# Planned order of shapes in attention, the last unit's sums on VectorE, and one expert per unit, in a two-layer transformer kernel

## The chip, the cores and the metric

The kernel runs on one core of a Trainium2 chip. The metric is device time in microseconds of one launch; lower is better. TensorE (PE) multiplies matrices, VectorE (DVE), ScalarE (ACT) and GpSimd (POOL) work on elements, SyncE (SP) and ACT issue most transfers. Each engine executes its own instructions in order.

## The reference, cut to what matters

Two layers over 2048 tokens of width 512, all in fp32.

```python
# layer 0
xn = layernorm(x)
q, k, v = heads(xn @ Wqkv + bqkv)              # 16 heads of 32
s = q @ k.T / sqrt(32) - slope[h] * (i - j)    # causal, slope[h] = 2 ** (-h / 2)
attn = softmax(s) @ v @ Wo + bo
e = argmax(softmax(xn @ Wg.T))                 # one of two experts per token
ffn = gelu(xn @ W0a.T + b0a) @ W0b.T + b0b if e == 0 else relu(xn @ W1a.T + b1a) @ W1b.T + b1b
x = x + attn + ffn                             # W0a, W1a: 1024 x 512
# layer 1
xn = layernorm(x)
x = x + lightning_attention(xn) + bitlinear_ffn(xn)   # linear attention with decays; 1408 wide, ternary weights
```

## The kernel before, in words

The kernel has four stages: attention of layer 0 (0 to 890 us), the experts of layer 0 (890 to 1157), the linear attention of layer 1 (1157 to 1552) and its ternary FFN (1552 to the end). The last two are the same in both kernels.

**Attention** has 16 units: four groups of four heads (`g`) by four blocks of 512 queries (`sb`). A unit has these parts on TensorE:
- `project` (L774, L886): queries, keys and values of the block. Q and K are split into two fp32r parts, written to DRAM and read back in another layout (SP, L834 and L847).
- `search` (L973): scores whose row maxima VectorE takes (L985). They are turned (L1039) and stored as `mr`.
- `attend`, once per block of 128 keys: `pick` (L1080) adds the negative maxima to four banks of PSUM, one for each head; `score` (L1090, on the diagonal also L1087) adds the scores; ScalarE takes the exponentials into `pT` (L1108); `weigh` (L1155) multiplies them with the values. The weighing of a key block comes after the scores of the next.
- `gather` (L1185): the exponentials of all key blocks are added up in `pT[0]`, on POOL. A product with ones (`sums`, L1202), two turns (L1237), a reciprocal and a multiplication divide the output.
- `out_proj` (L1305), in the last group only: the output projection, three groups as `others` and the last one as `late`; VectorE adds the result to the residual (L1314).

TensorE works in three shapes: `pick` uses 32 rows by 128 columns ("rows"), `weigh` and `sums` 128 rows by 32 columns ("columns"), the rest the whole 128x128 array ("full").

The order of attention is written by a planner when the kernel is built. `Plan` holds all parts as `Step`s, each with an engine, a duration, what it comes after, the PSUM banks or SBUF slots it takes, and a rank. TensorE's steps stand in streams (`own` for `attend`, `search`, `project`, `sums`, `others`, `late`, `extra`), in order within each. `choose` and `prefer` pick the next stream; `commit` sets the clock of the plan. `backlog` is the work waiting on VectorE, `searching` the work of searches already possible. There are seven PSUM banks beside `po`, and 18 SBUF slots (`homes`). An addition of `gather` may go to VectorE where POOL would start it later by more than `PATIENCE`. Steps up to the last weighing are then issued in the planned order on every engine (`manual_schedule`); those after it in an order that the compiler's scheduler chooses, mixed with the next stage.

**Experts.** `sort_tokens` gives each token a slot: tokens of expert 0 from the front, those of expert 1 from the end. Scatters (POOL) write the token numbers in this order to `sorted_tokens`; 18 gathers (L452, POOL) read them back to `take`. Nine units of 256 slots follow. Units that lie wholly among expert 0 or 1 use its weights; the slots of units above the border are shifted back by 256, so that the unit at the border is computed for either expert. Unit 0 is always expert 0, unit 8 always expert 1; the others load weights from `wa_all` and `wb_all`, copies of both experts behind each other in DRAM, at an index read from `second_i`. Per unit: gather and normalize the rows (L1557, L353; for units 0 and 1 as `xg_early` in attention), a first product (L1573, eight slices), ScalarE's activations (Relu L1580 and Gelu L1582, combined by VectorE in L1583; unit 0 has Gelu alone, L1577), a second product (L1587), the bias (L1589), a store to `expert_out`. After the last store POOL gathers its rows by `back` (L1694) for layer 1. While unit 0 is computed, `decay_tables` (L1489 to L1515) puts exponentials among its activations.

Of the kernel before, what the change touches and what calls it, by code (L numbers as in the profile page):

```python
# [9 lines left out]
F32 = mybir.dt.float32  # L10
I32 = mybir.dt.int32
# [6 lines left out]
P = 128  # L18
# [69 lines left out]
class Plan:  # L88
# [29 lines left out]
    def commit(self, step, at):  # L118
        if step.engine == "PE":
            shape = SHAPES.get(step.kind, "full")  # L120
            if shape != self.mode:
                at_work = step.took + (0.2 if self.mode == "rows" else 0.1)
                self.mode = shape
            else:
                at_work = step.took
        else:
            at_work = step.took
        end = at + at_work
# [44 lines left out]
    def prefer(self, ready, now):  # L173
# [12 lines left out]
        wanted = 1.2 if head is not None and head.kind in ("weigh", "pick") else 1.1  # L186
        search = ready.get("search")
        if search is not None and (search.kind == "turn" or backlog < wanted):
            return "search"
        if "sums" in ready and (head is None or self.mode == "columns" or head.kind == "pick"):  # L190
            return "sums"
        if "project" in ready and (ready["project"].kind == "middle" or self.searching() < 12.0):
            return "project"
        if "late" in ready and backlog < 1.0:
            return "late"
# [50 lines left out]
PATIENCE = 1.5  # L246
# [3 lines left out]
def block_kernel(  # L250
# [117 lines left out]

    dram = ctx.enter_context(tc.tile_pool(name="dram", bufs=1, space=bass.MemoryType.DRAM))
# [5 lines left out]
    expert_out = dram.tile([NU * LB, H], F32, tag="expert_out", name="expert_out")  # L375
# [4 lines left out]
    take = const.tile([P, NU, LB // P], I32, tag="take", name="take")  # L380
# [21 lines left out]
    def sort_tokens(pc, from_end):  # L402
# [22 lines left out]
        nc.vector.tensor_scalar(other, first0, -float(LB), float(LB), ALU.mult, ALU.add)  # L425
        nc.vector.tensor_tensor(other, other, pos, ALU.add)
# [3 lines left out]

        nc.vector.tensor_scalar(second[:, 0 : NU - 1], starts[:, 0 : NU - 1, 0], n0, None, ALU.is_gt)
        nc.vector.memset(second[:, NU - 1 : NU], 1.0)
        nc.vector.tensor_copy(second_i, second)
        shape = [P, NU, LB // P]
        slot = rt.tile(shape, F32, tag="slot", name="slot")
        nc.vector.tensor_scalar(slot[:, :, 0], second, -float(LB), None, ALU.mult)
        nc.vector.tensor_tensor(slot[:, :, 1], slot[:, :, 0], slots[:, :, 1], ALU.add)
        nc.vector.tensor_tensor(slot[:, :, 0], slot[:, :, 0], slots[:, :, 0], ALU.add)
        slot_i = rt.tile(shape, I32, tag="slot_i", name="slot_i")
        nc.vector.tensor_copy(slot_i, slot)  # L440
# [10 lines left out]
    def gather_take(u, k, slot_i):  # L451
        nc.gpsimd.indirect_dma_start(  # L452
            take[:, u, k : k + 1],
            None,
            sorted_tokens,
            bass.IndirectOffsetOnAxis(ap=slot_i[:, u, k : k + 1], axis=0),
        )

    starts = iota(const, [P, NU, 1], [[LB, NU], [0, 1]], 0, 0, "starts")
    slots = iota(const, [P, NU, LB // P], [[LB, NU], [P, LB // P]], 0, 1, "slots")  # L460
# [12 lines left out]
    with tc.tile_pool(name="psa", bufs=1, space=PSUM, reuse_waits="tile") as psa, tc.tile_pool(  # L473
# [582 lines left out]
        def attend(n, g, sb):  # L1056
# [120 lines left out]
            def gather(held_p):  # L1177

                for jb in range(1, nj):
                    cols = ds(first(jb), SB - first(jb))  # L1180

                    def step(jb=jb, cols=cols):
# [4 lines left out]
                    n_all = HPG * (SB - first(jb))  # L1187
                    added[jb] = add(
                        "POOL",
                        0.2 + 2.25e-3 * n_all,  # L1190
# [4 lines left out]
                        other=("DVE", 0.6 + 1.08e-3 * n_all),  # L1195
# [101 lines left out]
            def out_proj(il, groups):  # L1297
# [15 lines left out]
                def total():  # L1313
# [7 lines left out]
                    after=[d if last else others, wo["load"]] if il == 0 else [],  # L1321
# [22 lines left out]
        unit = {}  # L1344
        for n, (g, sb) in enumerate(units):
# [11 lines left out]
            for dst, src in copies[2 * (n - 4) : 2 * (n - 3)] if n >= 4 else []:  # L1357
                bulk(lambda dst=dst, src=src: nc.scalar.dma_start(out=dst, in_=src), after=[first_own[n]], rank=6)
# [17 lines left out]
        for i in range(NT):  # L1376
# [8 lines left out]
        taken = [  # L1385
            add("POOL", 1.0, lambda u=u, k=k: gather_take(u, k, t["slot_i"]), after=[step], rank=7, lag=7.0)
            for u in range(NU)
            for k in range(LB // P)
        ]
# [29 lines left out]
        def fetch_rows(i):  # L1419
            def step():  # L1420
                if i == 0:
                    early["xg"] = slot(held_g, "xg_early")
                u, k = divmod(i, LB // P)
                nc.gpsimd.indirect_dma_start(
                    early["xg"][:, i, :], None, x, bass.IndirectOffsetOnAxis(ap=take[:, u, k : k + 1], axis=0)
# [4 lines left out]
        def fetch_weights(k):  # L1430
            def step():
                w = slot(held_w[k], "wa_early", shape=[P, 2, F0])
                nc.sync.dma_start(out=w, in_=W0aT[ds(2 * k * P, 2 * P), :].rearrange("(c p) f -> p c f", p=P))
# [14 lines left out]
        for i in range(EARLY * (LB // P)):  # L1448
            fetched.append(
                add("POOL", 1.0, fetch_rows(i), after=[taken[i]] + used_up + fetched[-1:], rank=rank, lag=6.0, takes=[held_g] if i == 0 else [])  # L1450
            )
        weights = []
        for k in range(2):
            weights.append(add("SP", 0.62, fetch_weights(k), after=used_up + weights[-1:], rank=rank, takes=[held_w[k]]))
# [63 lines left out]
    with stage(4, 2, 2), tc.tile_pool(name="fc", bufs=1) as fc, tc.tile_pool(name="fw", bufs=2) as fw, tc.tile_pool(  # L1518
# [11 lines left out]
        for u in range(NU):  # L1530
            is0, is1 = firsts[:, u : u + 1], second[:, u : u + 1]
            wb = fw.tile([P, FC0, H], F32, tag="wb", name="wb")
            if u in (0, NU - 1):
                src_a, src_b = (W0aT, W0bT) if u == 0 else (W1aT, W1bT)
            else:
                e = nc.values_load(second_i[0:1, u : u + 1], engines=[mybir.EngineType.SP], min_val=0, max_val=1)
                src_a = wa_all[ds(e, 1)].rearrange("e k f -> (e k) f")
                src_b = wb_all[ds(e, 1)].rearrange("e f h -> (e f) h")
# [487 lines left out]
```

## Time and profile before

| | us |
|---|---|
| median of 3 runs | 1808.11 (1806.61 to 1808.33) |
| the profiled execution | 1807.18 |
| its span, first to last instruction | 1805.5 |
| attention | 0 to 890 |
| experts | 890 to 1157 |
| layer 1, linear attention | 1157 to 1552 |
| layer 1, FFN | 1552 to 1805.5 |

Durations of single instructions come from the profiled execution. Matrix instructions of fp32 appear in it as two passes, those of fp32r as one, so "x8" in a weighing is four instructions. Ends of TensorE's instructions are modelled; starts are recorded. In a row of the order of time the square bracket tells how long the engine was idle before it and what ended that.

### The profile page before, as it was taken

Reading aid. Unit: us, or ns where it says so; the run is one execution under the profiler, and the core shown is the slowest. Engines: PE = TensorE matmul, PEld = TensorE weight load, DVE = VectorE, ACT = ScalarE, POOL = GpSimd, SP = SyncE. Lnnn points to the kernel's source line nnn. Section 1 sums busy time; section 2 is a strip of 40 time slices with the busy share of each in tenths; the row PEclk is TensorE's granted clock in tenths of the full one; section 3 lists DMA queues with packets and bytes.
Section 4 is the critical chain, followed back from the end, with each engine's and each line's share of the span. In section 5 each row is a group of like instructions: output and inputs, shape, how many; then the busy total and the mean of one; then the engine's idle time right before and its main releaser. Section 6 shows DMA issues by size and latency. Waiting matters only on the chain.

```text
span 1805.5 us, 23633 instructions
## 1 busy us (share of the span) xinstructions
PE 1711.5 (95%) x9074; PEld 1086.6 (60%) x9074; DVE 892.0 (49%) x2116; ACT 697.0 (39%) x1223; POOL 805.2 (45%) x479
## 2 busy tenths in 40 slices
PE   5899999999999999899899999699999998799998
PEld 3656555555555555444556675476666664588886
DVE  3657656565666456621132231237766556652332
ACT  2344456555556556445152232123333331122221
POOL 8352879799967597879733130111111111000000
PEclk9899999999999999999999999899999998899999
DMA  7465243525442713301485453221210000310000
GB/s 207 152 198 158 54 94 101 140 53 147 119 145 88 213 39 100 111 1 65 128 302 188 169 175 111 73 76 60 73 48 30 13 1 1 98 49 6 24 24 24
DMA packets 90065, 173.94 MB, mean 96 GB/s; under 512 B 8944, under 2 KB 18176, under 8 KB 89696
## 3 DMA queue, kind: packets, MB, share of 16 engines
q1 hardware_dynamic: 74496, 133.33, 24.3%
q10 hardware_dynamic: 11088, 29.36, 4.8%
q0 software_dynamic: 4368, 9.75, 1.8%
q8 instruction: 71, 1.16, 0.3%
q14 instruction: 42, 0.34, 0.1%
HBM read 139.37 MB, written 41.43 MB: 100 GB/s over the span
## 4 chain that ended last, share of the span: by engine, by line
PE 44%; ACT 2%; DVE 2%; POOL 1%; issue 1%; DMA 1%; SPq 0%; DVEq 0%; ACTq 0%; POOLq 0%
PE ps_a L1950 9%; PE ps_c L1587 7%; PE ps_a L1715 7%; PE ps_a L1573 6%; PE ps_a L1857 3%; PE ps_a L1737 3%; PE ps_c L1935 2%; PE ps_b L1935 2%; PE ps_a L1814 1%; PE ps_a L1745 1%; PE ps_a L1811 1%; PE ps_a L1805 1%; DVE rms L1848 1%; PE ps_a L1845 1%; PE ps_a L1787 0%
## 5 line engine op out<-in xcount | busy, mean ns | idle before, releaser
L1185 POOL TENSOR_TENSOR pT<-pT 128x2048 f32<-128x2048 f32 (+3 forms) x144 | 553.1, 3843 | 106.9 <-ACT pT L1108 73.9
L985 DVE CUSTOM_DVE_ANT_0 bank<-bank,dist 128x512 f32<-128x512 f32 (+3 forms) x640 | 382.8, 631 | 183.4 <-PE bank L973 178.9
L1108 ACT ACTIVATE pT<-bank,kbias 128x512 f32<-128x512 f32 (+3 forms) x640 | 352.8, 624 | 179.8 <-PE bank L1090 156.5
L973 PE MATMUL bank<-Ks,Qs 128*128 128x512 f32 (+3 forms) x640 | 256.6, 440 | 8.1 <-DVE mx L985 6.8
L1090 PE MATMUL bank<-Qs,Ks 128*128 128x512 f32 (+3 forms) x640 | 213.9, 398 | 0.0
L973 PEld LDWEIGHTS bank<-Ks,Qs 128*128 128x128 f32 x640 | 113.8, 191 | 127.5 <-ACT pT L1108 48.0
L1950 PE MATMUL ps_a<-xs,w 128*128 128x512 f32 x704 | 168.2, 392 | 4.3 <-issue 4.3
L1950 PEld LDWEIGHTS ps_a<-xs,w 128*128 128x128 f32 x704 | 133.1, 189 | 33.0 <-issue 5.2
L1155 PE MATMUL po<-pT,v 128*32 128x512 f32 (+3 forms) x1280 | 150.7, 543 | 0.0
L1090 PEld LDWEIGHTS bank<-Qs,Ks 128*128 128x128 f32 x640 | 118.4, 190 | 32.6 <-issue 18.0
L774 PE MATMUL bank<-xnT,wqkv 128*128 128x512 f32 x256 | 127.7, 612 | 1.4 <-ACT xnT L714 1.4
L1587 PE MATMUL ps_c<-wb,hT 128*128 128x512 f32 x288 | 125.1, 592 | 0.0
L1715 PE MATMUL ps_a<-xn2T,wproj 128*128 128x256 f32 x512 | 118.4, 388 | 2.5 <-ACT xn2T L354 2.5
L1715 PEld LDWEIGHTS ps_a<-xn2T,wproj 128*128 128x128 f32 x512 | 96.9, 193 | 19.1 <-ACT xn2T L354 4.0
L1573 PE MATMUL ps_a<-xT,wa 128*128 128x256 f32 x448 | 98.3, 380 | 2.9 <-ACT xT L354 2.9
L1587 PEld LDWEIGHTS ps_c<-wb,hT 128*128 128x128 f32 x288 | 54.7, 190 | 65.0 <-issue 62.7
L1573 PEld LDWEIGHTS ps_a<-xT,wa 128*128 128x128 f32 x448 | 84.5, 190 | 15.1 <-ACT xT L354 3.9
L985 DVE DVE_READ_ACCUMULATOR2_ANT mx<- 128x1 f32 x640 | 90.7, 142 | 0.0
L1960 DVE TENSOR_TENSOR hf<-ps_a,s 128x512 f32<-128x512 f32 x44 | 30.4, 691 | 113.5 <-PE ps_a L1950 113.5
L1080 PE MATMUL bank<-mr,pick 32*128 32x512 f32 (+3 forms) x640 | 81.0, 464 | 5.5 <-DVE lo L815 2.8
L1836 POOL TENSOR_TENSOR sq<-og 128x512 f32<-128x512 f32 x16 | 16.9, 1059 | 152.4 <-DVE og L1831 152.4
L1848 DVE RECIPROCAL rms<-rms 128x512 f32<-128x512 f32 x16 | 53.6, 3351 | 57.5 <-ACT rms L1847 57.5
(228 smaller groups left out, 2209.2 us busy)
## 6 DMA issues: line engine op xcount, KB each, us to landing
Ks<-st SPq DMA_DIRECT2D x64, 256.0 KB, 4.6
Qs<-st SPq DMA_DIRECT2D x64, 256.0 KB, 4.5
wa<-wa_all SPq DMA_DIRECT2D x14, 1024.0 KB, 7.3
wb<-wb_all SPq DMA_DIRECT2D x14, 1024.0 KB, 7.9
xnT<-xn_dram ACTq DMA_DIRECT2D x12, 1024.0 KB, 5.7
raw<-in_L_ffn_w_dram SPq DMA_DIRECT2D x12, 704.0 KB, 4.1
st<-hi SPq DMA_DIRECT2D x32, 256.0 KB, 2.1
st<-lo SPq DMA_DIRECT2D x32, 256.0 KB, 2.0
```

Of the source, the lines that this page charges most:

```text
L774: nc.tensor.matmul(t["pp"], w3["w"][:, cc, ts(k, P)], xT["x"][:, cc, :], start=(cc == 0), stop=(cc == KC - 1),)
L973: nc.tensor.matmul(b["ps"][:, 0:w], un["Q"][:, hh, ts(il, P)], unit[n - sb + ch]["K"][:, hh, 0:w], start=True, stop=True,)
L985: nc.vector.tensor_tensor_reduce(out=b["ps"][:, 0:w], in0=b["ps"][:, 0:w], in1=c["dist"][:, ds(off, w)], scale=1.0, scalar=-3e38, op0=ALU.add,
L1080: nc.tensor.matmul(ps[hh][:, cols], c["pick"][hp, :], un["mr"][hp, cols], start=True, stop=False)
L1090: nc.tensor.matmul(ps[hh][:, cols], unit[n - sb + jb // TPS]["K"][:, hh, ts(jb % TPS, P)], un["Q"][:, hh, cols], start=False, stop=True,)
L1108: nc.scalar.activation(pT[jb][:, hh, cols], ps[hh][:, cols], AF.Exp, bias=c["kbias"][:, h, rel : rel + 1], scale=SLOPES[h],)
L1155: nc.tensor.matmul(t["po"][ts(hh, HD), cols], unit[n - sb + jb // TPS]["v"][:, jb % TPS, ts(hh, HD)], pT[jb][:, hh, cols], start=(jb == 0) ...
L1185: engine.tensor_tensor(acc, acc, pT[jb][:, :, cols], ALU.add)
L1573: nc.tensor.matmul(ph[:, 0:LB], wa[c][:, ts(f, P)], xT[:, c, :], start=(c == 0), stop=(c == KC - 1))
L1587: nc.tensor.matmul(po, hT[:, f, ts(k, P)], wb[:, f, :], start=(f == 0), stop=(f == FC0 - 1))
L1715: nc.tensor.matmul(pp[:, ts(i, LB)], w[:, c, ts(g, P)], self.xT[:, c, :], start=(c == 0), stop=(c == KC - 1),)
L1950: nc.tensor.matmul(pp, w[:, c, ts(f, P)], xs[i][:, c, :], start=(c == 0 and i == 0), stop=(c == KC - 1 and i == 1),)
```

## The change

1. *The planner.* A change of shape on TensorE costs 0.2 us in the plan where it leads to the full shape and 0.09 otherwise (before: 0.2 where it left rows, else 0.1). Where TensorE stands in columns and the next own step is a pick that can start within `WAIT` (0.4), nothing of another shape is put before it. The thresholds at which searches, projections and late products are preferred are others, and `PATIENCE` is 4.0 instead of 1.5.
2. *The last unit's additions* are given to VectorE.
3. *The experts.* Eight units of 256 slots are computed for one expert each, the one to which the slot in their middle belongs. The 128 slots at the border that this leaves out are a last unit of one tile. `sort_tokens` finds that tile (`meet`), its expert, and the place of its tokens (`back`). `take` is read by one load on SP and one gather. All units, unit 0 too, load weights at an index and have both activations.

```diff
     def commit(self, step, at):
+        end = at + step.took
         if step.engine == "PE":
+
             shape = SHAPES.get(step.kind, "full")
             if shape != self.mode:
-                at_work = step.took + (0.2 if self.mode == "rows" else 0.1)
+                end += 0.2 if shape == "full" else 0.09
                 self.mode = shape
...
-        wanted = 1.2 if head is not None and head.kind in ("weigh", "pick") else 1.1
+        wanted = 1.8 if head is not None and head.kind == "weigh" else 0.9
         search = ready.get("search")
+        if self.mode == "columns" and head is not None and head.kind == "pick":
+
+            at = self.start(head)
+            if at < now + WAIT:
+                return "own" if own is not None else None
...
-        if "project" in ready and (ready["project"].kind == "middle" or self.searching() < 12.0):
+        if "project" in ready and (ready["project"].kind == "middle" or self.searching() < 45.0):
             return "project"
-        if "late" in ready and backlog < 1.0:
+        if "late" in ready and backlog < 0.6:
...
-PATIENCE = 1.5
+PATIENCE = 4.0
+WAIT = 0.4
...
+                    times = {"POOL": 0.2 + 2.25e-3 * n_all, "DVE": 0.6 + 1.08e-3 * n_all}
+                    engine = "DVE" if n == len(units) - 1 else "POOL"
                     added[jb] = add(
-                        "POOL",
-                        0.2 + 2.25e-3 * n_all,
+                        engine,
+                        times[engine],
...
-                    after=[d if last else others, wo["load"]] if il == 0 else [],
+                    after=[d if last else others, wo["load"], loaded[-1]] if il == 0 else [],
...
-        taken = [
-            add("POOL", 1.0, lambda u=u, k=k: gather_take(u, k, t["slot_i"]), after=[step], rank=7, lag=7.0)
-            for u in range(NU)
-            for k in range(LB // P)
-        ]
+        taken = add("SP", 0.62, load_take, after=[step], rank=7, lag=12.0)
+        taken_last = add("POOL", 1.0, lambda: gather_take(t["slot_i"]), after=[step], rank=7, lag=7.0)
...
-                nc.sync.dma_start(out=w, in_=W0aT[ds(2 * k * P, 2 * P), :].rearrange("(c p) f -> p c f", p=P))
+                src = weights_of(0)[0]
+                nc.sync.dma_start(out=w, in_=src[ds(2 * k * P, 2 * P), :].rearrange("(c p) f -> p c f", p=P))
...
-            if u in (0, NU - 1):
-                src_a, src_b = (W0aT, W0bT) if u == 0 else (W1aT, W1bT)
-            else:
-                e = nc.values_load(second_i[0:1, u : u + 1], engines=[mybir.EngineType.SP], min_val=0, max_val=1)
-                src_a = wa_all[ds(e, 1)].rearrange("e k f -> (e k) f")
-                src_b = wb_all[ds(e, 1)].rearrange("e f h -> (e f) h")
+            src_a, src_b = weights_of(u)
+            n = LB if u < NU - 1 else P
...
                     nc.tensor.matmul(
-                        ph[:, 0:LB], wa[c][:, ts(f, P)], xT[:, c, :], start=(c == 0), stop=(c == KC - 1)
+                        ph[:, 0:n], wa[c][:, ts(f, P)], xT[:, c, 0:n], start=(c == 0), stop=(c == KC - 1)
                     )
-                if u == 0:
-                    nc.scalar.activation(hT[:, f, :], ph[:, 0:LB], AF.Gelu, bias=ba[0][:, f : f + 1])
-                    continue
...
-            for k in range(LB // P):
+            for k in range(n // P):
                 po = ps_c()
```

The new functions:

```python
    def load_take():
        nc.sync.dma_start(
            out=take[:, 0 : NT], in_=sorted_tokens[:, 0].rearrange("(t p) -> p t", p=P)
        )

    def weights_of(u):

        e = nc.values_load(second_i[0:1, u : u + 1], engines=[mybir.EngineType.SP], min_val=0, max_val=1)
        return wa_all[ds(e, 1)].rearrange("e k f -> (e k) f"), wb_all[ds(e, 1)].rearrange("e f h -> (e f) h")
```

In `sort_tokens`, ten more operations on tiles of 128x1 and 128x16 find the border:

```python
        nc.vector.tensor_scalar(full, ends, n0, None, ALU.is_le)
        nc.vector.tensor_reduce(meet[:, 0:1], full, AX.X, ALU.add)
...
        nc.vector.scalar_tensor_tensor(other, away[0], behind, pos, ALU.mult, ALU.add)
        nc.vector.tensor_copy(back, other)
...
        nc.vector.tensor_scalar(second[:, 0 : NU - 1], middles, n0, None, ALU.is_gt)
```

## The prediction

> **What bounds the kernel now.** I read the page first, then busy time by stage, then TensorE's instructions in order of time, then the chain of waits.
>
> ```profile
> PE 1711.5 (95%) x9074; PEld 1086.6 (60%) x9074; DVE 892.0 (49%) x2116; ACT 697.0 (39%) x1223; POOL 805.2 (45%) x479
> ```
>
> In stretches of 100 us (sum, then busy us of PE, PEld, DVE, ACT, POOL; granted clock, DMA share, GB/s):
>
> ```profile
> 600.00:700.00 100.00, 100.00 (x611) 56.27 (x611) 55.17 (x171) 59.88 (x110) 74.04 (x26) 1.00 0.48 140
> 700.00:800.00 100.00, 92.22 (x502) 46.47 (x501) 55.77 (x159) 47.72 (x88) 77.78 (x29) 0.97 0.15 53
> 1000.00:1100.00 100.00, 97.64 (x347) 62.86 (x346) 26.25 (x59) 25.96 (x56) 23.30 (x21) 1.00 0.49 174
> ```
>
> The first two lie in attention (0 to 890 us), the third among the experts (890 to 1157). TensorE sets the time in both; no other engine passes 78% here. But "busy" hides what it is busy with, so the next view is TensorE's order of time (start, length, line). First a key block with two searches (L973) between its weighing (L1155) and its picks (L1080), then one without:
>
> ```profile
> 617.82 0.39 PE L973 MATMUL bank<-Ks,Qs 128*128 128x512 f32 x1
> 618.05 0.39 PE L1090 MATMUL bank<-Qs,Ks 128*128 128x512 f32 x1
> ...
> 619.08 1.07 PE L1155 MATMUL po<-pT,v 128*32 128x512 f32 x8
> 620.08 0.73 PE L973 MATMUL bank<-Ks,Qs 128*128 128x512 f32 x2
> 620.74 0.51 PE L1080 MATMUL bank<-mr,pick 32*128 32x512 f32 x4
> ...
> 783.49 1.07 PE L1155 MATMUL po<-pT,v 128*32 128x512 f32 x8
> 784.48 0.51 PE L1080 MATMUL bank<-mr,pick 32*128 32x512 f32 x4
> ```
>
> Read starts, not lengths. A search among scores takes 0.23 us (617.82 to 618.05). From weighing to picks it is 1.66 us with two searches and 0.99 without: 0.67 for 0.46 us of work. So a visit of the full 128x128 shape between columns (128x32) and rows (32x128) costs 0.20 us beyond its work. The same 0.20 comes out with one search there.
>
> The end of attention (POOL's order of time, then TensorE's), and the chain of waits at the experts' last unit:
>
> ```profile
> 819.91 48.94 POOL L1185 TENSOR_TENSOR pT<-pT 128x2048 f32<-128x2048 f32 x12 [1.01 <-ACT pT L1108]
> ...
> 879.56 0.66 PE L1237 MATMUL bank<-ident,rec 128*128 128x128 f32 x4 [0.19 <-ACT rec L1244]
> 882.15 1.11 PE L711 MATMUL bank<-ident,xn 128*128 128x128 f32 x4 [1.93 <-POOL xn L704]
> 884.22 1.12 PE L711 MATMUL bank<-ident,xn 128*128 128x128 f32 x4 [0.96 <-POOL xn L704]
> 885.13 5.40 PE L1305 MATMUL bank<-wo,aoT 128*128 128x512 f32 x8
> ```
> ```profile
> 1129.06 14.08 PE ps_a L1573 x64
> 1143.14 13.75 PE ps_c L1587 x32
> 1158.00 5.30 DMA raw<-in_L_ffn_w_dram
> ```
>
> GpSimd adds the last unit's exponentials until 868.9, though its last weighing ends at 860.3. What hangs on the sum leaves TensorE short of work: 0.19 + 1.93 + 0.96 idle, and 1.8 more in the last line, whose eight passes need 3.4 us at 0.43 each.
>
> **The change, part by part.**
>
> *Shape changes.* Counted in the two built orders of TensorE, attention has 629 changes of shape before and 522 after; picks stand directly behind a weighing 28 times before and 129 times after. Visits of the full shape (its exits to rows or columns) fall from 125 + 172 = 297 to 30 + 166 = 196. The matrix products themselves are the same in number and size. 101 visits by 0.20 us: **-20 us**, while TensorE is what attention waits for.
> The cover: the searches removed from that place now stand among scores or ahead of the weighing, in runs as before (runs of three or more: 13 before, 12 after). A pick needs four of seven banks, each set free by an exponential (ACT, 2.42 us for four). A block with two searches takes TensorE about 2.9 us, so ACT is ready; blocks with at most two searches are 37 before and 46 after. Nearest row for the wait: in blocks without any search the trace has two rounds in 3.55 us where starts without waiting add up to 3.45. 0.1 us on all 129 direct picks would give back 13; on the few thin ones 1 to 2. I take **+2** for new waits.
>
> *VectorE adds the last unit.* 15 additions leave POOL (62.8 us there, 4.58 for each full one). VectorE has no 2048-wide row; its 128x512 addition of two SBUF tiles takes 0.69 and its 1408-wide reduction 1.61, so about 2.3 us for a full one and some 31 for all. TensorE's blocks of that unit come every 2.5 us or more, so the additions keep pace and the sum is there with the last weighing. In the new order ones-product, transposes and early transposes then stand ahead of eight output products of 2.6 us, so every round trip has a cover. The 4.9 us of idling go: **-4.9**; bounds -4.9 and 0, since the residual rows for those products are issued on ACT's queue only near the end of the unit and land 5.4 us later. Output products now queue behind additions on VectorE: at most 2.3 us late each, with seven banks to bridge it.
> [...] The trace has this row of VectorE's update of S (min/median/max ns), whose inputs both lie in SBUF:
>
> ```profile
> L1839 DVE SCALAR_TENSOR_TENSOR S<-S,cdec,kv x8: 339/342/1155, 1211.4 to 1234.6; 128x128 f32<-128x128 f32 x8
> ```
>
> The 1.16 us cases are those that meet POOL's 1.06 us square (L1836). [...] In the new order VectorE's first addition stands behind the earlier unit's final product, which needs POOL's last addition. What is left on POOL is three normalizations of 2.08 us[...]. [...] I take nothing.
>
> *Eight units and a tile.* The ninth unit is half as wide. Its first product has 64 passes of 128 instead of 256 columns, 16 passes of the second go, and four of eight transposes. Could weight loads (0.19 us each) bound the narrow passes? No: a row with new weights on every pass and 128 columns is
>
> ```profile
> 605.83 3.73 PE L886 MATMUL bank<-wqkv,xnT 128*128 128x128 f32 x32
> ```
>
> 0.115 us a pass. So 13.8 becomes 7.2, 13.75 becomes 6.9, 1.04 becomes 0.5: **-14.2**. ACT's two activations per slice (1.03 us at 256 columns) shrink too and stay under the 0.9 us of a slice, or near it. The store, the gather and the wait of 13 us behind it are the same.
>
> *Unit 0 becomes like the others.* It gains eight Relus (0.56) and eight VectorE combinations (0.48). VectorE takes them in order with the statistics of the next rows, which wait for gathers: those began at 903.2, 906.0, 911.6, 914.1 and 916.6. The last three slices stand behind the fifth, so the second product, which began at 910.7 and wants them by 915 to 917, has to wait: **+3**, bounds -1 and +6.
>
> *The rest at nothing.* Ten more tiny operations in the sort (0.15 us each) on a VectorE at 56 to 63%. POOL loses 17 gathers of 1 us. SP gains a load of 2048 four-byte entries ahead of the last group's weights and Q/K reads: the nearest row, the gate's 4 KB in eight-byte pieces, landed in 10.8 us; those reads (4.6 us) run three units ahead of use, which is the cover. Without it up to 10 us, once. SP also gets two more register loads ahead of a K read, and unit 0's weights now come from the copies, written long before. PATIENCE is inert: in both orders no other addition goes to VectorE.
>
> **Sum.** -20 + 2 - 4.9 - 14.2 + 3 = -34. The profiled execution took 1807.2 us (span 1805.5); the median of the runs is 0.9 above it. So 1773 for such an execution, 1774 for the median.
>
> **The rivals.** Differences under 0.2% (3.6 us) count as no change, about what a measurement of this kernel can tell.
> - *The picks wait instead.* Every direct pick pays 0.1 us for its banks. For it: the thin blocks above, and two picks of 1.37 and 1.39 us instead of 0.5 near 819 and 822. Against: those blocks had no search in them. Gain 34 - 11 - 3 more for a late load: 1788. Chance 0.17.
> - *More goes.* The 6.8 us at 761.7 in which TensorE waited for VectorE's maxima (L985) go as well, and unit 0 costs nothing: 1774 - 6.8 - 3 - 2 = 1762. Against: the new order has a run of 15 searches at that place, at 0.65 us each on VectorE. Chance 0.14.
> - *The change does not do what it says in attention*, because shape changes are not what is waited for there: only the tile and unit 0 count, -14 + 3: 1797. Against: TensorE at 100% in most stretches. Chance 0.04.
> - *Slower[...].* [...] Against: the order above. Chance 0.05.
>
> **How the numbers follow.** The likeliest case, 0.60, is 1774, itself 1767 to 1782. 1762 to 1789 takes in the second and third ends and leaves out less than 2 in 10. All cases but the last are faster: 0.94; within 0.2% 0.01; slower 0.05.
>
> **What would show it.** Right: starts from weighing to picks of 0.99 us nearly everywhere; attention ending near 868 instead of 890; VectorE additions of 2.3 us ended before the last weighing; no idle above 0.5 us between there and the experts; a last unit of 15 us instead of 29. Wrong: picks of 0.6 us or longer as a rule, ones-product waiting for VectorE, additions of 4 us or more, searches waiting for Q or K behind the new load, or experts' unit 0 longer than 40 us.

## The result, and the profile after

The changed kernel takes 1794.14 us (median of four runs, 1790.62 to 1795.74) against 1808.22 for the kernel before on the same chip (1806.61 to 1809.84): ratio 0.9919, 95% interval 0.9902 to 0.9937. That is 14 us faster where 34 were forecast, above the range of 1762 to 1789. The profiled execution took 1794.14 us, its span is 1792.4 (1805.5 before). By stages of the two traces:

| stage (profiled) | before | after | difference | forecast |
|---|---|---|---|---|
| attention, to the first expert product | 890.4 | 887.7 | -2.7 | -22.9 |
| experts, to the last second product | 266.5 | 257.4 | -9.1 | -11.2 |
| what follows | 648.6 | 647.3 | -1.3 | 0 |

So the experts came out nearly as forecast, and attention did not. Two of the stretches shown of before, as they are now (stretch, sum, then busy us of PE, PEld, DVE, ACT, POOL; granted clock, DMA share, GB/s):

```profile
600.00:700.00 100.00, 99.08 (x615) 55.00 (x612) 50.30 (x162) 63.80 (x119) 83.42 (x29) 1.00 0.29 90
...
1000.00:1100.00 100.00, 98.36 (x345) 62.87 (x344) 24.35 (x54) 25.28 (x54) 20.71 (x18) 1.00 0.50 176
```

TensorE is still what sets the time. Its order of time shows that the change does what it says: picks (L1113) start 0.99 us behind a full weighing (L1188).

```profile
592.93 1.06 PE L1188 MATMUL po<-pT,v 128*32 128x512 f32 x8
593.92 0.44 PE L1113 MATMUL bank<-mr,pick 32*128 32x384 f32 x4
```

What TensorE waited for between 100 and 840 us, by the view of waits (in total, times, longest), first in the kernel before:

```profile
PE bank L973 <- DVE mx L985: 6.8, 1, 6.8
PE bank L1080 <- DVE lo L815: 2.8, 1, 2.8
```

then in the changed kernel:

```profile
PE bank L1113 <- DVE mx L1018: 4.2, 1, 4.2
PE bank L1072 <- POOL mq L1060: 3.5, 2, 2.8
PE bank L1113 <- ACT mr L1076: 2.3, 2, 2.1
PE bank L1272 <- ACT rec L1264: 1.8, 2, 1.0
```

The longest wait of before (6.8) is gone. The one of 2.8 stood behind VectorE's sort of the tokens; behind the longer sort of the changed kernel it is 4.2 (first line). New are round trips at the ends of units: the turn of the maxima (L1072), of the sums (L1272), the picks for the row maxima (mr). All lines of these views come to 12.5 us before and 16.9 after.

The end of attention in the changed kernel. First VectorE's last full addition of the last unit and the one that completes the sum (start, length, line):

```profile
831.72 2.29 DVE L1218 TENSOR_TENSOR pT<-pT 128x2048 f32<-128x2048 f32 x1 [1.54 <-ACT pT L1141]
...
838.89 0.69 DVE L1218 TENSOR_TENSOR pT<-pT 128x512 f32<-128x512 f32 x1 [0.45 <-ACT pT L1141]
```

TensorE in order of time:

```profile
841.87 1.04 PE L1237 MATMUL bank<-pT,ones 128*32 128x512 f32 x8
...
857.06 1.11 PE L744 MATMUL bank<-ident,xn 128*128 128x128 f32 x4 [8.77 <-POOL xn L737]
857.97 1.92 PE L1340 MATMUL bank<-wo,aoT 128*128 128x512 f32 x2
859.68 22.13 PE L1340 MATMUL bank<-wo,others 128*128 128x512 f32 x48
```

and POOL:

```profile
840.62 0.56 POOL L331 DMA_DIRECT2D bo<-in_L_attn_bo_dram  x1
851.13 1.26 POOL L1559 TENSOR_TENSOR bo<-bo,bias_row 128x512 f32<-128x512 f32 x1 [9.95 <-DMA bo<-in_L_attn_bo_dram]
...
854.93 2.08 POOL L737 TENSOR_SCALAR xn<-xg_early,mv,rstd 128x512 f32<-128x512 f32 x1
```

VectorE's sum is there at once (ones-product at 841.87, behind the last weighing). But POOL, freed of its additions, reaches the load of bo at 840.6 and stands still until it lands at 851.1. The last early row's normalization (L737) is queued behind three additions that wait for this load, and TensorE waits for that row: 8.77 us. Then it runs at half clock for a while (granted 0.50 up to 862.4; two products in 1.92 us instead of 1.02).

The experts' unit 0 and the last unit, TensorE in the changed kernel:

```profile
887.65 10.52 PE L1604 MATMUL ps_a<-xT_early,wa_early 128*128 128x256 f32 x48
903.01 5.41 PE L1604 MATMUL ps_a<-xT_early,wa_early 128*128 128x256 f32 x16 [4.83 <-ACT ge L1610]
...
913.50 13.12 PE L1615 MATMUL ps_c<-wb,hT 128*128 128x512 f32 x26 [1.91 <-DVE hT L1611]
...
1130.79 7.41 PE L1604 MATMUL ps_a<-xT,wa 128*128 128x128 f32 x64 [0.68 <-ACT xT L357]
1138.04 7.03 PE L1615 MATMUL ps_c<-wb,hT 128*128 128x512 f32 x16
```

The last unit's products take 14.4 us instead of 27.8, as worked out. Unit 0 takes 38.8 us instead of 33.9. The wait for ScalarE in it (4.83) stood there before as well:

```profile
905.27 5.41 PE L1573 MATMUL ps_a<-xT_early,wa_early 128*128 128x256 f32 x16 [4.39 <-ACT hT L1577]
```

The waits for VectorE (0.33 and 1.91) are new.

### The profile page after: what moved, and what is told of

The parts are those of the page before. It is cut to its first block, busy times and chain, and to the rows that moved or that the text cites. A ratio compares the mean times of both kernels' runs of the same rounds, so it can differ in the third digit from the quotient of the medians.

```text
span 1792.4 us, 23648 instructions
## 1 busy us (share of the span) xinstructions
PE 1685.1 (94%) x9054; PEld 1083.2 (60%) x9054; DVE 927.9 (52%) x2144; ACT 692.6 (39%) x1228; POOL 726.0 (41%) x449
## 3 DMA queue, kind: packets, MB, share of 16 engines
q8 instruction: 71, 1.16, 0.3%
## 4 chain that ended last, share of the span: by engine, by line
PE 43%; issue 3%; ACT 2%; DVE 2%; DMA 1%; POOL 1%; SPq 0%; DVEq 0%; ACTq 0%; POOLq 0%
PE ps_a L1978 9%; PE ps_a L1743 7%; PE ps_c L1615 6%; PE ps_a L1604 6%; PE ps_a L1885 4%; PE ps_a L1765 3%; PE ps_c L1963 2%; PE ps_b L1963 2%; PE ps_a L1842 1%; PE ps_a L1773 1%; PE ps_a L1839 1%; PE ps_a L1833 1%; DMA xg<-in_L_attn_x_dram,take 1%; DVE rms L1876 1%; PE ps_a L1815 0%
## 5 line engine op out<-in xcount | busy, mean ns | idle before, releaser
L1218 POOL TENSOR_TENSOR pT<-pT 128x2048 f32<-128x2048 f32 (+3 forms) x129 | 490.7, 3809 | 114.6 <-ACT pT L1141 94.9
L1006 PE MATMUL bank<-Ks,Qs 128*128 128x512 f32 (+3 forms) x640 | 255.5, 437 | 1.7 <-DVE mx L1018 1.5
L1006 PEld LDWEIGHTS bank<-Ks,Qs 128*128 128x128 f32 x640 | 116.3, 191 | 60.5 <-issue 22.1
L1188 PE MATMUL po<-pT,v 128*32 128x512 f32 (+3 forms) x1280 | 151.3, 540 | 0.5 <-ACT pT L1141 0.5
L807 PE MATMUL bank<-xnT,wqkv 128*128 128x512 f32 x256 | 134.8, 634 | 2.0 <-ACT xnT L747 2.0
L1615 PE MATMUL ps_c<-wb,hT 128*128 128x512 f32 x272 | 120.4, 600 | 2.2 <-DVE hT L1611 2.2
L1113 PEld LDWEIGHTS bank<-mr,pick 32*128 32x128 f32 x640 | 33.1, 182 | 121.6 <-ACT pT L1141 55.8
L1604 PE MATMUL ps_a<-xT,wa 128*128 128x256 f32 (+1 forms) x448 | 91.6, 365 | 2.9 <-ACT xT L357 2.9
L1604 PEld LDWEIGHTS ps_a<-xT,wa 128*128 128x128 f32 x448 | 79.7, 190 | 13.4 <-ACT xT L357 3.8
L1113 PE MATMUL bank<-mr,pick 32*128 32x512 f32 (+3 forms) x640 | 79.7, 461 | 7.1 <-DVE mx L1018 4.2
```

The lines of the kernel that those rows point to most:

```text
L807: nc.tensor.matmul(t["pp"], w3["w"][:, cc, ts(k, P)], xT["x"][:, cc, :], start=(cc == 0), stop=(cc == KC - 1),)
L1006: nc.tensor.matmul(b["ps"][:, 0:w], un["Q"][:, hh, ts(il, P)], unit[n - sb + ch]["K"][:, hh, 0:w], start=True, stop=True,)
L1113: nc.tensor.matmul(ps[hh][:, cols], c["pick"][hp, :], un["mr"][hp, cols], start=True, stop=False)
L1188: nc.tensor.matmul(t["po"][ts(hh, HD), cols], unit[n - sb + jb // TPS]["v"][:, jb % TPS, ts(hh, HD)], pT[jb][:, hh, cols], start=(jb == 0) ...
L1218: engine.tensor_tensor(acc, acc, pT[jb][:, :, cols], ALU.add)
L1604: nc.tensor.matmul(ph[:, 0:n], wa[c][:, ts(f, P)], xT[:, c, 0:n], start=(c == 0), stop=(c == KC - 1))
```

## The experiments

Three theories. **A**: a visit of the full shape costs its 0.20 us and TensorE is what attention waits for, so the saving is real, but the new plan brings waits of its own that take it back. **B**: shape changes are not what attention waits for. **C**: the saving is whole, and the end of attention alone ate it. "Visits" are counted in the built orders, "attention ends" is read from one trace each (first expert product), times are medians. Three kernels of this study with the same attention end it at 878.9, 875.9 and 879.4 us, so differences of some 3 us between single traces tell nothing.

### The parts alone and in pairs

Each of these is the kernel before with the lines of the change that belong to the parts named, and no other line.

Planner alone (its rule, costs and thresholds):

> The kernel before with the planner's part of the change alone (shape costs, thresholds, the rule that lets a ready pick follow a weighing). In the built order TensorE has 520 changes of shape and 195 visits of the full shape in attention, as in the changed kernel (522 and 196), against 629 and 297 before; the rows' normalizations stand ahead of the bias rows on POOL. Theory A (the 20 us of shape changes are saved, but the new order opens waits of its own at the ends of units, and some of these are followed by a stretch at half clock, which take some 12 to 17 back): attention ends 3 to 8 us earlier than before, 1800 to 1805, and TensorE's idle time before the last weighing is longer than before. Rival B (shape changes are not what attention waits for): no change, 1806 to 1810, and no stage is shorter. Rival C (the saving is whole, and only the end of attention of the changed kernel eats it): 1786 to 1790.

VectorE's additions alone:

> The kernel before with the second part alone: VectorE adds the last unit's exponentials. Shape changes are as before (628 and 297 visits). By the prediction's sum: -4.9, so 1803. Theory A and rival C alike: two rows' normalizations still stand behind the sum with the bias row on POOL, and this row's place in SBUF comes free when it did in the changed kernel, so TensorE waits 5 to 9 us for it instead of 4.9 for the sum: 1806 to 1814. Rival B: as the prediction, 1803.

Experts alone:

> The kernel before with the third part alone: eight units of one expert each and one tile. Shape changes are nearly as before (636 and 302 visits). By the prediction's terms -14.2 and +3, so 1797; with the changed kernel's unit 0 (38.8 us against 34.0 before) instead of +3, -9.4, so 1799. Theory A: 1797 to 1801. Rival B, in which this part is the whole gain: 1793 to 1796.

The two without the planner:

> The second and third part of the change together, with the planner as before (303 visits of the full shape in the built order, 25 picks directly behind a weighing). If the parts add up, the two that were run alone give 1808.9 + 0.0 - 6.6 = 1802; the planner's part would then be worth -8 in the changed kernel (1794), although it cost 22 alone. Theory A: 1799 to 1806, so that the planner's part is worth 5 to 12 once the last unit's sum is out of its way. Rival C (its saving of 20 is whole there): 1810 to 1815. Rival B (worth nothing): 1792 to 1796.

The two without the experts:

> The kernel before with the first and second part (new planner, VectorE adds the last unit), without the experts' part. 195 visits, 129 direct picks; the rows' normalizations all stand ahead of the bias rows on POOL. If the second part is worth what the first cost at the end (16.9 us of waiting, and of 23.9 us at half clock behind it about 12 lost): 1831 - 29 = 1802 (1798 to 1806). If the parts add up as they did alone (+22 and 0): 1831.

| parts | visits | attention ends | time | ratio to before, 95% |
|---|---|---|---|---|
| planner | 195 | 912.0 | 1831.2 | 1.0129 (1.0113 to 1.0146) |
| VectorE | 297 | 894.1 | 1809.0 | 1.0003 (0.9994 to 1.0012) |
| experts | 302 | 895.7 | 1802.3 | 0.9963 (0.9950 to 0.9975) |
| planner, VectorE | 195 | 882.2 | 1798.8 | 0.9937 (0.9920 to 0.9954) |
| VectorE, experts | 303 | 883.9 | 1790.7 | 0.9891 (0.9872 to 0.9910) |
| all three | 196 | 887.7 | 1794.1 | 0.9919 (0.9902 to 0.9937) |

No theory had foreseen the first row: the planner's part alone, with a third of the visits gone, costs 22 us. The end of attention with the planner alone, TensorE in order of time:

```profile
880.58 1.71 PE L1158 MATMUL po<-pT,v 128*32 128x256 f32 x16
899.21 1.93 PE L1205 MATMUL bank<-pT,ones 128*32 128x512 f32 x8 [16.92 <-POOL pT L1188]
```

In this plan the last weighing has nothing left behind it, and GpSimd's sum comes 16.9 us later; what follows runs at half clock (granted 0.50 from 890 to 910; 1.93 us for a ones-product of 1.04). With VectorE's additions this goes, 32 us for a part that alone gains nothing. So the parts do not add up: +22, 0 and -6.6 alone, -14 together. And the kernel without the planner's part is 3.4 us faster than the changed one (the intervals touch). The experts alone shorten their stage from 266.5 to 255.5 us: the forecast -11.2, nearly to the point; of their gain 5 us are lost again at the end of attention, where waits for early rows grew from 2.9 to 7.8 us.

### What the end of attention cost

The changed kernel, with the loads of the three bias rows held back until the last early row is done (called the 1783 kernel below):

```diff
+        behind = early["xT"][EARLY - 1][:, 0, LB - 1 : LB]
+            t = fc.tile([P, ap.shape[0]], F32, tag=tag, name=tag)
+            nc.gpsimd.tensor_copy(t[:, 0:1], behind)      # for bo, b0b, b1b
             nc.gpsimd.dma_start(out=t, in_=ap.partition_broadcast(P))
```

> The changed kernel, with the loads of the three bias rows made to wait for the last early row (one column of it is copied into them first). On TensorE, VectorE and ScalarE the order is the same; on POOL the last early normalization no longer stands behind the sum with the bias row. Theory A and rival C: the 8.8 us in which TensorE waits for that normalization go, and of the half-clock stretch behind them (10.2 us, 4 to 5 us lost) most: 1780 to 1786. If instead the idle time only moves (to the next round trip, or to unit 0, where the rows now come later): 1790 to 1795.

Measured: 1783.1 (ratio to before 0.9859, 0.9839 to 0.9878), 11 us faster than the changed kernel, and the fastest of this study. POOL normalizes the last early row at 848.75 instead of 854.93. TensorE in this kernel:

```profile
850.88 0.66 PE L744 MATMUL bank<-ident,xn 128*128 128x128 f32 x4 [1.44 <-POOL xn L737]
851.38 1.02 PE L1340 MATMUL bank<-wo,aoT 128*128 128x512 f32 x2
852.24 20.76 PE L1340 MATMUL bank<-wo,others 128*128 128x512 f32 x48
```

The wait falls from 8.77 to 1.44 us, and the half clock behind it is gone (granted 1.00 from 850 to 870; 1.02 and 20.76 us instead of 1.92 and 22.13, with the transposes 2.7 us). Attention ends at 878.8. That is the cause of this loss, shown. It refutes C too: with this loss gone, the gain is 26 and not 34.

### What a shape change costs

In the 1783 kernel a search is put back between a weighing and its pick, after the planner has run, where its bank is free there:

```diff
+                    if free:
+                        order.insert(pes[1], order.pop(pes[k]))   # pes[1]: the pick
```

> The changed kernel with the bias rows behind the early rows (1783), and with one edit behind the planner: where a pick follows a weighing and one of TensorE's next searches has a bank that nothing between them uses, this search is taken out of its place and put between the two. The same instructions, the same plan otherwise; visits of the full shape go from 196 to 302, direct picks from 129 to 23. Theory A (a visit costs 0.20 us and TensorE is what attention waits for): +21, so 1804 (1799 to 1808). Rival B (shape changes are not waited for): 1781 to 1786.

Measured: 1805.4 (0.9981, 0.9972 to 0.9989) against 1783.1, +22.3 for 106 visits: 0.21 us each. In the two traces attention ends 15.5 us later (894.4 and 878.9), although 27 us of it are at half clock instead of 41; with half of that difference, an estimate of what it hides, 22 come out again. The waits between 100 and 840 us do not grow (15.0 us after, 17.7 before the searches are put back). The same block, first in the 1783 kernel (from the start of a weighing to the next, 3.29 us):

```profile
595.48 1.06 PE L1188 MATMUL po<-pT,v 128*32 128x512 f32 x8
596.48 0.44 PE L1113 MATMUL bank<-mr,pick 32*128 32x384 f32 x4
...
598.77 1.06 PE L1188 MATMUL po<-pT,v 128*32 128x512 f32 x8
```

then with the search (L1006) put back (3.49 us):

```profile
604.32 1.07 PE L1188 MATMUL po<-pT,v 128*32 128x512 f32 x8
605.32 0.38 PE L1006 MATMUL bank<-Ks,Qs 128*128 128x256 f32 x1
605.63 0.44 PE L1113 MATMUL bank<-mr,pick 32*128 32x384 f32 x4
...
607.81 1.06 PE L1188 MATMUL po<-pT,v 128*32 128x512 f32 x8
```

Theory B has fallen: the price is right, and in this plan it is paid in full.

### Where the saving goes

The old planner with the mended end (the kernel of the second and third part, with the edit of the bias rows):

> The second and third part with the planner as before (1790.7), and the bias rows behind the early rows as in the 1783 kernel. 303 visits. Its end of attention had two waits for rows' normalizations (1.9 and 2.6 us, then 6.8 at half clock): these go, or most of them, -3 to -6: 1785 to 1788. Then the planner's part, with the same end of attention, is worth 2 to 5 (1783) instead of the 20 of its shape changes. If the waits there have another cause: 1790.

Measured 1791.6 (0.9906, 0.9890 to 0.9923): the mending does nothing here. A wait of 2.6 us for an early row becomes 1.4, but one of 1.9 ahead of it and one of some 4 us in unit 0 stay. So with the same edit at the end, the planner's part is worth 8.5 us (1791.6 to 1783.1) where its 107 visits are worth 22. Of the 13.5 us that are missing, the view of waits shows 9: between 100 and 840 us its lines come to 8.6 with the old planner and to 17.7 in the 1783 kernel.

The same plan, with picks moved ahead of searches and nothing planned anew:

```diff
+            order[w + 1 : at + 1] = first + [p] + rest       # p: the pick, w: the weighing
```

> np_tail with one edit behind the planner: where searches stand between a weighing and its picks, the picks go ahead of them if nothing between touches their banks. Visits go from 303 to 234, direct picks from 25 to 94; nothing is planned anew. Theory A (the saving is real, the losses come from the new plan): 69 x 0.20 = -14, less what the earlier picks wait for their banks (0 to 5): 1771 to 1778. Rival (picks that come earlier wait for exponentials, so that the saving comes back at once): 1783 to 1788.

Measured 1801.9 (0.9954, 0.9940 to 0.9969): 10 us slower, with 69 visits less. The rival's direction was right, and its loss was larger than it said. A block of the old plan, TensorE in order of time:

```profile
264.79 1.06 PE L1185 MATMUL po<-pT,v 128*32 128x512 f32 x8
265.78 0.73 PE L1003 MATMUL bank<-Ks,Qs 128*128 128x512 f32 x2
266.44 0.50 PE L1110 MATMUL bank<-mr,pick 32*128 32x512 f32 x4
...
268.49 1.06 PE L1185 MATMUL po<-pT,v 128*32 128x512 f32 x8
```

and with its pick ahead:

```profile
264.42 1.06 PE L1185 MATMUL po<-pT,v 128*32 128x512 f32 x8
265.41 0.55 PE L1110 MATMUL bank<-mr,pick 32*128 32x512 f32 x4
265.89 0.74 PE L1003 MATMUL bank<-Ks,Qs 128*128 128x512 f32 x2
266.47 0.39 PE L1120 MATMUL bank<-Qs,Ks 128*128 128x512 f32 x1
267.36 0.50 PE L1003 MATMUL bank<-Ks,Qs 128*128 128x512 f32 x1 [0.50 <-DVE mx L1015]
...
268.72 1.06 PE L1185 MATMUL po<-pT,v 128*32 128x512 f32 x8
```

From weighing to weighing 3.70 becomes 4.30. The pick takes its four banks of seven first, two searches come behind it, and the third finds no bank: it waits for VectorE to finish a maximum, and VectorE got its first search of this block 0.5 us later than before. The trace has 18 such waits, 7.3 us in all. The picks wait as well: 25 of 58 full ones directly behind a weighing take over 0.1 us more than the 0.43 from their start to the next instruction, and all picks together 8 us more than in the old plan. So in this plan a search between weighing and pick cost a shape change and was worth more: it kept VectorE fed while the pick's banks came free. The sum does not close: 15 us lost and 10 us slower leave 5 of the 14 that 69 visits should have saved, and the trace does not tell where the others went. A plan made with the rule puts its searches elsewhere. In the changed kernel 1 of 86 such picks is late, and searches wait 1.1 us for maxima; but it has other waits.

Which part of the planner makes them? Each kernel below is the 1783 kernel with one or more of its constants as they were.

Projections held back as before:

```diff
-        if "project" in ready and (ready["project"].kind == "middle" or self.searching() < 45.0):
+        if "project" in ready and (ready["project"].kind == "middle" or self.searching() < 12.0):
```

> The kernel with the bias rows behind the early rows (1783), with one of the planner's constants as it was: projections go ahead while fewer than 12 us of searches are open, not 45. Visits of the full shape stay at 195 and direct picks at 134; TensorE's order falls into fewer groups (1841 instead of 1885). If the new waits come from projections that go too far ahead (searches and the end of a unit then have nothing beside them), attention gets 5 to 12 us shorter: 1771 to 1778. If they come from the direct picks, or from any new order: 1780 to 1788.

Without the rule:

```diff
-        if self.mode == "columns" and head is not None and head.kind == "pick":
-            at = self.start(head)
-            if at < now + WAIT:
-                return "own" if own is not None else None
```

> The same kernel (1783) without the rule that lets a pick follow a weighing when it could start within 0.4 us; the other constants are the new ones. Visits go from 196 to 277, direct picks from 129 to 48. If the waits that eat the saving come from the rule itself: 81 visits x 0.20 = +16 and as much back, 1780 to 1785. If they come from the other constants: 1795 to 1800.

Old thresholds of VectorE's backlog:

```diff
-        wanted = 1.8 if head is not None and head.kind == "weigh" else 0.9
+        wanted = 1.2 if head is not None and head.kind in ("weigh", "pick") else 1.1
```

> The same kernel (1783) with the threshold of VectorE's backlog below which a search is put ahead as it was (1.2 and 1.1 us instead of 1.8 and 0.9). Visits 198, direct picks 130, groups 1864. If long runs of searches ahead of weighings (1.8) make the waits: 1773 to 1779. If any new order has its own waits: 1779 to 1788.

All three thresholds old (both edits above, and `backlog < 1.0` for late products instead of 0.6):

> np_tail planned anew with the new shape costs and the rule that lets a ready pick follow a weighing, all other thresholds as before. 197 visits, 133 direct picks. If the thresholds changed beside the rule bring the waits: -15 to -20 against np_tail, 1767 to 1773. If any new plan has waits of its own: 1778 to 1788.

The sort as a generator with four stops, and a step of the plan for each piece:

```diff
-        placed = add("DVE", 4.5, place, after=[counted], uses=[held], rank=7)
+        placed = add("DVE", 2.4, place, after=[counted], uses=[held], rank=7)
+        for took in (1.1, 1.4, 1.4, 1.2):
+            placed = add("DVE", took, place, after=[placed], rank=7)
```

> The same kernel (1783) with VectorE's sort (39 small operations, 10 us in one step) as five steps of the plan, between which searches' maxima can come. The order changes: 201 visits of the full shape, 127 direct picks. Theory A: the 4.2 us in which a pick waits near 296 and the 6.8 us at half clock behind it (3.4 lost) go: 1775 to 1779. Rival (the planner's order is so sensitive that another wait comes in its place): 1779 to 1789.

| kernel | visits | attention ends | time | ratio to before, 95% |
|---|---|---|---|---|
| all new (bias rows mended) | 196 | 878.8 | 1783.1 | 0.9859 (0.9839 to 0.9878) |
| projections ahead under 12 us of searches | 195 | 875.6 | 1785.6 | 0.9866 (0.9844 to 0.9887) |
| sort in five steps | 201 | 878.1 | 1785.0 | 0.9857 (0.9837 to 0.9876) |
| old backlog thresholds | 198 | 886.6 | 1793.9 | 0.9918 (0.9891 to 0.9945) |
| rule and costs new, thresholds old | 197 | 891.9 | 1804.9 | 0.9978 (0.9971 to 0.9985) |
| thresholds new, no rule | 277 | 903.6 | 1807.5 | 0.9977 (0.9965 to 0.9988) |

Five plans with nearly the same visits (195 to 201) lie 22 us apart. The rule is worth some 23 us beside the new thresholds (2.4 us below the kernel before without it, 25.8 with it), and loses 13 beside the old ones (1791.6 to 1804.9). Taking one threshold back gains nothing. So "any new order has its own waits" is what held; none of the constants tried is the cause alone. What these plans share is a wait that the kernel before did not have between 100 and 840 us, the turn of a unit's maxima for POOL: 3.5 us in the changed kernel, 4.1 in the 1783 kernel, 5.6 with the sort in steps, 7.9 with projections held at 12, 9.0 with the rule and old thresholds, 14.0 with the old backlog thresholds; without the rule it is 1.1. The sort in five steps did not do what it was made for: in its trace no maximum stands between the pieces, two copies of the sort took 3.3 us each (see the last section), and the wait behind it is 4.2 us again.

### Two trials elsewhere

Products into TensorE's wait behind the last unit, ahead of the linear attention's blocks:

```diff
+        pw = ps_a()
+        for i in range(28):
+            nc.tensor.matmul(pw, ident, wk[:, i % KC, :], start=True, stop=True)
```

> The same kernel (1783) with 28 products of 128 x 512 into a bank that nobody reads (0.43 us each, 12 us in all), put into TensorE's wait of 13.3 us behind the last expert unit. They compute nothing that is used. If idle time is what brings the half clock, the 20.5 us at half clock behind this wait shrink to 7 or less, and 6 to 9 us go: 1774 to 1777. If the half clock comes from something else, or the next waits (1.9 and 0.7 us) bring it anyway: 1781 to 1784. If the products end too late: up to 1790.

Measured 1788.0 (0.9870, 0.9848 to 0.9891): a product of this kind is two passes, 24.2 us for all, and ended 11 us too late. But it shows what it was to show. Behind the last unit without the products (the same columns as above, the clock is the third number from the end):

```profile
1150.00:1160.00 10.00, 7.44 (x20) 5.77 (x20) 7.39 (x16) 2.46 (x3) 4.37 (x6) 0.51 0.44 151
```

and with them:

```profile
1150.00:1160.00 10.00, 9.28 (x35) 5.78 (x34) 3.63 (x10) 2.36 (x3) 2.68 (x4) 1.00 0.34 116
```

With 0.72 us of idle time in this stretch instead of 2.56, and no wait of 13.3 us ahead of it, the granted clock is 1.00 and not 0.51; the next 64 passes (L1751) took 14.08 us instead of 17.12.

Half as many of them, and the decay tables behind unit 1:

```diff
+        nc.gpsimd.tensor_copy(diff[:, 0:1], behind)     # ahead of the iota into diff
-            if u == 2:
-                decay_tables()
+            if u == 1:
+                decay_tables(hT[:, FC0 - 1, 0:1])
```

> The same kernel (1783) with two edits at places far apart. The decay tables are made to wait for unit 1 (one column of its hidden layer is copied into them first), so that ScalarE no longer stops in unit 0 for a table whose input POOL makes late, nor loads Exp and Gelu tables in turn: TensorE's waits of 4.8, 0.5 and 1.7 us there go, and 3.4 us at half clock behind them, unit 0 at 29 to 32 us instead of 38.8: -6 to -9. And in the wait of 13.3 us behind the last expert unit, TensorE does 14 products of 0.86 us that nobody reads (28 of them were 24 us and ended 11 us too late): the 20.5 us at half clock go, in which 3.0 us of work were lost: -3, unless the products end too late. Together 1771 to 1774. If the wait in unit 0 only moves to the next gather: 1779 to 1781.

Measured 1790.8 (0.9876, 0.9844 to 0.9909): no gain in either place. Unit 0's waits moved to its second product (2.9 and 3.4 us for the hidden layer), the experts took 258.9 us. The products ended where they should (1150.3), but a second wait of 2.3 us followed and 6.8 us at half clock with it. Unit 0 is left open.

## Why the prediction was wrong, step by step

- *Shape changes, -20*: the price was right (0.20 forecast, 0.21 measured), and so was the count.
- *"I take +2 for new waits"*: this is the step that failed most. Attention ahead of its end came out at -9.3 (-2.7 less the +6.6 of the next step); if 101 visits saved 21 us, that leaves +12 for new waits, give or take the 3 us between traces. The argument asked only whether the pick finds its banks, and there it was right for this plan (1 late in 86). The row it leaned on (two rounds in 3.55 us) does not stand in the trace of before in that form; blocks without a search take 2.55 us there, and those at 818 and 821 take 3.42 and 4.29. It took for granted that the removed searches cost nothing in their new places, and did not ask what they had done in the old one. The waits view shows 4.4 of the 12; up to the last weighing 40.9 us are at half clock instead of 37.5, which is at most 1.7 more; the rest is spread over starts that no view names, and is not settled.
- *The sort, at nothing*: "ten more tiny operations" did not cover it. VectorE's sort took 9.9 us (289.38 to 299.24) instead of 4.3 (223.47 to 227.76), 3.2 of them lost in one copy beside an addition of GpSimd (last section), and the wait behind it grew from 2.8 to 4.2 us. This is part of the 4.4.
- *VectorE's additions, -4.9 and "no idle above 0.5 us"*: the mechanism was right (2.29 us an addition, 2.3 forecast; sum there with the last weighing). The trace of before even had such a row, contrary to what was said: four additions of 128x2048 at L1928, 2.28 us each. What comes next was not asked: POOL, being early, meets a load that is not, and a row stands behind it. Before, the waits there came to 4.9 us; after, 8.8 idle and 2.7 at half clock: +6.6. The cover named for the round trips (eight output products) was there, and was placed behind the wait. The half clock had no term of its own in the sum, and one row was misread for it: the last 1.8 of the 4.9 us were not idle time. TensorE was busy throughout, at about half clock (columns as above, kernel before):

```profile
885.00:889.00 4.00, 4.00 (x7) 1.77 (x6) 0.91 (x2) 0.59 (x1) 1.61 (x2) 0.53 0.93 264
```

- *Tile, -14.2*: right. *Unit 0, +3 (bounds -1 and 6)*: +4.9, inside its bounds; the wait behind VectorE was as described (1.9 and 0.3 us), with products at half clock behind it (granted 0.50 from 913.7 to 917.0), and the wait for ScalarE, which the kernel before had too, grew by 0.4.
- *The rivals*: the slower end did not come; no addition took over 2.29 us. "Not what is waited for" gave a time near the measured one (1797) for a reason that the run with searches put back has refuted. None of them held the mechanism that decided, a plan with its own waits.
- The parts were summed as if independent. VectorE's part was worth 0 alone and 32 with the planner's; a sum of single terms cannot hold that.

## What to carry to other kernels

An instruction between two others may cost a shape change (0.21 us here) and still be worth its place: before taking it away, ask which engine it feeds and which buffer it frees, and who waits when that comes later. When a planner lays out the work, a saving of a kind of step is not a saving of time; judge two plans by their waits and run each part with and without the others, since parts of +22, 0 and -6.6 made -14. And when an engine is relieved, look at the next thing in its queue: here it was a load that had to land before a row that TensorE needed.

## What the runs showed of the hardware

- Idle time of TensorE cost more than its length. In the changed kernel it waits 2.75 us, from 433.3 to 436.0 (L1072, for POOL), and the clock is halved at the end of the wait and behind it (columns as above):

```profile
434.00:436.00 2.00, 0.00 (x0) 0.00 (x0) 0.00 (x0) 0.00 (x0) 1.25 (x3) 0.94 0.00 0
436.00:439.00 3.00, 2.97 (x7) 1.91 (x8) 0.76 (x2) 1.75 (x3) 3.00 (x1) 0.50 0.01 0
439.00:449.00 10.00, 10.00 (x64) 6.69 (x66) 5.63 (x14) 1.76 (x3) 9.73 (x4) 0.99 0.51 139
```

That stretch at half clock lasts 3.4 us (435.8 to 439.2). In the same trace the one from 299.2, begun within a wait of 4.2 us, lasts 6.8 us; the one from 725.9, behind 2.1 us, lasts 3.4; the one from 852.2, begun within the wait of 8.77 us, lasts 10.2. The granted clock is 0.50 in each. The 1783 kernel's wait of 1.44 us was followed by none (1.00 from 850 to 870).
- A copy of two columns on VectorE, in the sort, took 3.36 us. It began 0.2 us after an addition of GpSimd, which ran from 290.43 to 293.96, and ended with it:

```profile
290.63 3.36 DVE L416 COPY run<-run 128x2 f32<-128x2 f32 x1
```

POOL at that time:

```profile
290.43 3.53 POOL L1218 TENSOR_TENSOR pT<-pT 128x1536 f32<-128x1536 f32 x1
```

The same copy in the kernel before, with no addition beside it, and in the kernel with the rule and old thresholds, beside a shorter addition (227.39 to 228.68):

```profile
224.18 0.17 DVE L412 COPY run<-run 128x2 f32<-128x2 f32 x1
227.58 1.13 DVE L416 COPY run<-run 128x2 f32<-128x2 f32 x1
```

Over all 18 traces it took 0.17 us in the eleven where no addition of GpSimd ran beside it, and in the other seven it ended within 0.03 us of the addition's end. VectorE's update of S in the prediction's row, which has two inputs where the copy has one, took up to 1.16 us instead of 0.34 beside POOL's square of 1.06. The last unit's full additions had nothing beside them, since GpSimd stood idle from 784.2 to 839.4 us, and took 2.28 to 2.29 us each. Why the copy lasts as long as the addition was not shown; no run was made to try it apart.
